# A 64-token chunk of the feed-forward block, split by output channels over both column halves of TensorE

## The chip, the cores and the metric

The kernel runs on one core of one Trainium2 chip. The metric is the device time of one execution, in microseconds (us), as the median of a few runs. Times from the profile come from one more execution, taken with the hardware profiler.

## What is computed

The input is 32 images of 56 x 56 positions with 128 channels, all float32. Two layers follow each other, each added to its input. The first is windowed attention (7 x 7 windows, shifted by 3, four heads) on a group-normalised input. The second is a Fourier layer: cosine transforms along both directions, 32 modes kept and mixed, transformed back, and then a feed-forward block on every token. The change touches the end of the second layer alone. Cut to what matters:

```
def _feedforward(x, W1, b1, W2, b2):          # W1: 128 x 512, W2: 512 x 128
    h = jax.nn.relu(x @ W1 + b1)
    return h @ W2 + b2

x = x + _L0_conv_ref(_gn(x), ...)             # attention
x = x + feedforward(forward_fourier(_gn(x)))  # Fourier layer; x here is the residual
```

## The kernel before, in words

The program walks over "cycles". A cycle does one row of eight windows (7 lines of an image) in each stage of the attention, and beside it one step of the Fourier layer of an image whose attention is over. An image takes eight cycles, and the stages of several rows and two images overlap in one cycle. The orders of TensorE (PE), ScalarE (ACT), VectorE (DVE) and GpSimd (POOL) are written out by hand: they run what the functions below emit, in the order of the program. SyncE's queue (SP) issues nearly all DMAs; its order is set by the framework's scheduler, which places each DMA by an estimate of when it can go, so it may move when the program changes.

An image has 3136 tokens. The feed-forward block takes them in seven groups, `FF_GROUPS = (512, 512, 512, 512, 512, 320, 256)`, in the cycles that `FF_AT` names, one group to a cycle. In this text the groups are numbered from 0; group 5 is the one with 320 tokens. Three functions do a group:

- `ff_in` (L816) issues the load of the residual `res` from the scratch tensor `scr` in DRAM, 128 tokens to a column block (L822), and of a last part of fewer tokens, if there is one (L826). It then does the first layer: for each of the four blocks f of 128 hidden units, TensorE makes W1's block times the tokens in a PSUM bank, and ScalarE writes it with bias and ReLU to `hid` (L833). The hidden units lie on the partitions, the tokens along the free axis.
- `ff_bias` (L836) has POOL add the output bias `b2sb` to `res` (L840).
- `ff_out` (L847) does the second layer into one PSUM bank `pf`. For each chunk of 128 tokens and each f, the stationary operand is `hid` (128 hidden units x 128 tokens) and the moving operand is W2's block `wff2[:, f]` (128 x 128 channels). The tokens come out on the partitions. VectorE adds `pf` and `res` (L868), and SP stores the result (L880, L881, L888).

All matmuls of this block go through `halved`:

```
    def halved(dst, lhsT, rhs, start=True, stop=True):
        for p in range(0, dst.shape[0], P // 2):
            ps = slice(p, min(p + P // 2, dst.shape[0]))
            nc.tensor.matmul(dst[ps], lhsT=lhsT[:, ps], rhs=rhs, start=start, stop=stop)
```

It cuts the stationary operand into two of 64 columns, one for each half of the array's columns; the halves' results lie on partitions 0 to 63 and 64 to 127. All matmuls of this kind stand under line L113 in the profile.

Group 5 has two chunks of 128 tokens and one of 64. The chunk of 64 needs only one piece in `halved`, on partitions 0 to 63: four matmuls of 64 stationary columns and 128 moving columns.

In a cycle with a feed-forward group, TensorE runs around `ff_out` in this order: attention values (L546), scores (L477), the transform back (L789), the value product (L455), `ff_out` (L113), the attention's projection (`attn_project`, L591), q and k of the next row (L113, tile `xw`), and the next group's `ff_in` (L113, tile `xf`). VectorE follows with the output add (L868), the projection's residual add (L599), the softmax sums (L507, L509), and the statistics (L616, L629; the squares in between are ScalarE's L628). One other group of matmuls matters for comparison: `fourier_stats` (L649) multiplies a fixed 128 x 128 matrix, cut into halves of 64 columns, with 64 moving columns, twice per image.

The image normalisation (`image_norm`, L362) uses a small VectorE tile `gmeans` (L383), which the change also touches.

Of the kernel before, what the change touches and what calls it, by code (L numbers as in the profile page):

```python
# [9 lines left out]
F32 = mybir.dt.float32  # L10
AF = mybir.ActivationFunctionType
ALU = mybir.AluOpType
AX = mybir.AxisListType

P = 128
S = 56
C = 128
WS = 7
SS = 3
# [5 lines left out]
NT = S * S  # L25
NM = 32
FF = 512
NF = FF // P
# [5 lines left out]
JP = 64  # L34
HB = 512

HALVES = (slice(0, P // 2), slice(P // 2, P))
# [3 lines left out]
FF_GROUPS = (HB, HB, HB, HB, HB, 320, 256)  # L41
# [6 lines left out]
def swin_fourier_kernel(  # L48
# [20 lines left out]
    nc = tc.nc  # L69
    NB = x.shape[0]  # L70

    const = ctx.enter_context(tc.tile_pool(name="const", bufs=1))
    big = ctx.enter_context(tc.tile_pool(name="big", bufs=1))
    work = ctx.enter_context(tc.tile_pool(name="work", bufs=2))
    small = ctx.enter_context(tc.tile_pool(name="small", bufs=2))
# [6 lines left out]
    def attn_bank():  # L82
        return bank("pa", 4)

    def conv_bank():
        return bank("pc", 4)
# [22 lines left out]
# [5 lines that stand above are left out]
# [153 lines left out]
    b1sb = const.tile([P, NF], F32, tag="b1sb", name="b1sb")  # L267
    wff2 = const.tile([P, NF, C], F32, tag="wff2", name="wff2")
    b2sb = const.tile([P, C], F32, tag="b2sb", name="b2sb")

    def ff_weights():
        nc.sync.dma_start(wff1, W1)
        nc.sync.dma_start(b1sb, b1.rearrange("(f p) -> p f", p=P))
        nc.sync.dma_start(wff2, W2.rearrange("(f p) o -> p f o", p=P))
        nc.sync.dma_start(b2sb, b2.partition_broadcast(P))

    mhalf = const.tile([P, 1], F32, tag="mhalf", name="mhalf")
    nc.gpsimd.memset(mhalf, -0.5)
# [83 lines left out]
    def image_norm(im):  # L362

        GR = C // 16

        def average(out, src):
            sums = small.tile([P, GR], F32, tag="gsums", name="gsums", bufs=2)
            nc.vector.tensor_reduce(
                sums, src.rearrange("p (g c) -> p g c", c=4), axis=AX.X, op=ALU.add
            )  # L370
            nc.vector.tensor_scalar(
                out.rearrange("p (g c) -> p g c", c=4),
                sums.unsqueeze(2).to_broadcast([P, GR, 4]),
                0.25,
                None,
                ALU.mult,
            )

        nc.vector.bn_aggr(stat[:, 0:2], im.st)

        turned = small.tile([P, 32], F32, tag="turned", name="turned", bufs=2)
        nc.vector.transpose(turned, stat)
        mean = small.tile([P, 2, 32], F32, tag="gmeans", name="gmeans", bufs=2)  # L383
        average(mean[:, 0], turned)
        yield
        nc.vector.tensor_tensor(turned, turned, mean[:, 0], ALU.subtract)
        nc.vector.tensor_tensor(turned, turned, turned, ALU.mult)
        average(mean[:, 1], turned)
        back = small.tile([P, 2, 32], F32, tag="back", name="back", bufs=2)
        nc.vector.transpose(  # L390
            back.rearrange("p k c -> p (k c)"), mean.rearrange("p k c -> p (k c)")
        )
        gm = back[:, 0, 0:1]

        im.mean = small.tile([P, 1], F32, tag="mean0", name="mean0")
        nc.vector.tensor_scalar(im.mean, gm, -1.0, None, ALU.mult)

        ve = small.tile([P, 1], F32, tag="ve", name="ve")
        nc.vector.scalar_tensor_tensor(
            out=ve, in0=back[:, 0, 1:2], scalar=1e-5, in1=back[:, 1, 0:1], op0=ALU.add, op1=ALU.add  # L400
        )
        rstd = small.tile([P, 1], F32, tag="rstd0", name="rstd0")
        nc.gpsimd.tensor_tensor(rstd, ve, mhalf, ALU.pow)
        im.w = work.tile([P, 3 * C], F32, tag="wn", name="wn")
        im.bias = small.tile([P, 5], F32, tag="bqkv", name="bqkv")
        yield
        nb = small.tile([P, 1], F32, tag="nb0", name="nb0")
        nc.vector.scalar_tensor_tensor(
            out=nb, in0=gm, scalar=-1.0, in1=rstd, op0=ALU.mult, op1=ALU.mult
        )  # L410
        nc.scalar.mul(im.w, wqkv, rstd)  # L411
        yield
        pb = attn_bank()
        halved(pb[:, 0:1], wqkv[:, 2 * C :], nb)
        nc.vector.tensor_copy(im.bias[:, 2:3], pb[:, 0:1])
        yield
# [399 lines left out]
    def ff_in(im, g):  # L816
        t0, n = sum(FF_GROUPS[:g]), FF_GROUPS[g]
        k, last = n // P, n % P
        xff = im.xf.rearrange("p r w -> p (r w)")
        scr_tok = im.scr.rearrange("h w c -> (h w) c")  # L820
        res = work.tile([P, 4, C], F32, tag="res", name="res")
        nc.sync.dma_start(  # L822
            res[:, :k], scr_tok[t0 : t0 + k * P].rearrange("(n p) c -> p n c", p=P)
        )
        if last:
            nc.sync.dma_start(res[:last, k], scr_tok[t0 + k * P : t0 + n])  # L826
        im.res = res
        im.hid = []
        for f in range(NF):
            ph = conv_bank()  # L830
            halved(ph[:, :n], wff1[:, f * P : (f + 1) * P], xff[:, t0 : t0 + n])
            hf = work.tile([P, HB], F32, tag="hid", name="hid", bufs=NF)
            nc.scalar.activation(hf[:, :n], ph[:, :n], AF.Relu, bias=b1sb[:, f : f + 1])  # L833
            im.hid.append(hf)

    def ff_bias(im, g):  # L836
        k, last = FF_GROUPS[g] // P, FF_GROUPS[g] % P
        for c0, c1, m in ((0, k, P), (k, k + 1, last)):
            if m:
                nc.gpsimd.tensor_tensor(  # L840
                    im.res[:m, c0:c1],
                    im.res[:m, c0:c1],
                    b2sb[:m].unsqueeze(1).to_broadcast([m, c1 - c0, C]),
                    ALU.add,
                )

    def ff_out(im, g):  # L847
        t0, n = sum(FF_GROUPS[:g]), FF_GROUPS[g]
        k, last = n // P, n % P
        res = im.res  # L850
        out_tok = out[im.b].rearrange("h w c -> (h w) c")
        chunks = [P] * k + ([last] if last else [])
        pf = conv_bank()
        for c, m in enumerate(chunks):
            for f in range(NF):
                halved(
                    pf[:m, c * C : (c + 1) * C],
                    im.hid[f][:, c * P : c * P + m],
                    wff2[:, f],
                    start=(f == 0),  # L860
                    stop=(f == NF - 1),
                )
        parts = [(0, k, P), (k, k + 1, last)]
        if im.b == NB - 1 and g == len(FF_GROUPS) - 1:
            parts = [(c, c + 1, m) for c, m in enumerate(chunks)]
        for c0, c1, m in parts:
            if m:
                nc.vector.tensor_tensor(  # L868
                    res[:m, c0:c1],
                    pf[:m, c0 * C : c1 * C].rearrange("p (n c) -> p n c", c=C),  # L870
                    res[:m, c0:c1],
                    ALU.add,
                )

        c = 0
        while c < len(chunks):
            m = chunks[c]
            o = t0 + c * P + SS * S
            if o < NT < o + m:
                nc.sync.dma_start(out_tok[o:NT], res[: NT - o, c])  # L880
                nc.sync.dma_start(out_tok[: o + m - NT], res[NT - o : m, c])  # L881
                c += 1
                continue
            e = c + 1
            while len(parts) == 2 and e < len(chunks) and chunks[e] == m and (o >= NT or o + (e + 1 - c) * m <= NT):
                e += 1
            o %= NT
            nc.sync.dma_start(  # L888
                out_tok[o : o + (e - c) * m].rearrange("(n p) c -> p n c", p=m), res[:m, c:e]
            )  # L890
            c = e

    images = {}  # L900
# [78 lines left out]
    def behind_max(cycle):  # L979
        if cycle % NWR == NWR - 1:  # L980
            norm_step(cycle)
        turn(cycle)
        for im, c in fourier(cycle):
            if c == 0:
                next(im.stats, None)
            if c in FF_AT:
                ff_bias(im, FF_AT.index(c))
        last, j = row(cycle - 4)
        if last and j < NWR - 1:
            add_sums(last, j)  # L990
        next_groups(cycle)
# [115 lines left out]
    def last_out(cycle):  # L1107
        for im, c in fourier(cycle):
            if c in FF_AT:
                ff_out(im, FF_AT.index(c))  # L1110
# [34 lines left out]
    def first_rows(cycle):  # L1145
# [47 lines left out]
        if cycle == 8:  # L1193
            ff_weights()
# [116 lines left out]
```

## Time and profile before

| what | value |
|---|---|
| median of 3 runs | 3284.2 us (3283.5 to 3284.87) |
| the profiled execution's own time | 3282.72 us |
| its span, from first to last instruction | 3280.9 us |
| mean granted TensorE clock | 0.991 |
| busy share of TensorE, its weight loads, VectorE, ScalarE, POOL | 96, 73, 80, 64, 72% |
| moved by DMA | 448.39 MB, 137 GB/s |

Each row of the groups names a line of the kernel, the engine, the operation, the tiles written and read with their shapes, and the count; then the total busy time and the mean duration of one; then how long the engine sat idle just before these instructions, and what ended that. PE stands for matmuls, PEld for TensorE's weight loads, which run beside them. A matmul's duration is that of a pipeline and longer than the distance to the next one, so distances between starts say more than durations. A float32 matmul appears as two matmul records and two weight-load records. In the chain of waits, "issue" is time in which the engine waited for nothing that the profile shows. Queue q8 in the page carries TensorE's instructions.

### The profile page before, as it was taken

To read this page: it belongs to the slowest core of one execution; us is meant where nothing else is said; L and a number is where in the kernel's file an instruction comes from. 1 tells how busy PE (TensorE), PEld (TensorE's weight loads), DVE (VectorE), ACT (ScalarE), POOL (GpSimd) and SP (SyncE) were. 2 spreads that over 40 slices of the span, in tenths; PEclk is the share of its full clock that TensorE was granted. 3 is DMA by queue.
4 is the path that set the end of the run, shared out by engine and by line. 5 is a ranking of instruction groups with operands and counts; after the bars stand their busy time and mean duration, and the time that the engine had idled before them with its cause. 6 is when DMAs were issued, how large, how long until landed. Compare 5 with 4: busy or idle time off the path is not lost.

```text
span 3280.9 us, 151050 instructions
## 1 busy us (share of the span) xinstructions
PE 3154.8 (96%) x65408; PEld 2394.1 (73%) x65408; DVE 2637.5 (80%) x5066; ACT 2100.4 (64%) x3680; POOL 2346.8 (72%) x2634
## 2 busy tenths in 40 slices
PE   4689999999999999999999999999999999999999
PEld 3467777777777777777777777777777777777776
DVE  8788888888888888888888888888888888888751
ACT  3456766666766666666666766666666666666663
POOL 7777777777777677777777777777777777777741
PEclk9799999999999999999999999999999999999999
DMA  6546556565556555656556656656565656565453
GB/s 115 106 119 147 137 138 144 136 143 146 137 134 142 137 142 143 142 135 146 137 144 145 141 134 143 137 141 144 136 140 136 146 131 146 140 143 136 121 140 96
DMA packets 1168157, 448.39 MB, mean 137 GB/s; under 512 B 520106, under 2 KB 1137628, under 8 KB 1167492
## 3 DMA queue, kind: packets, MB, share of 16 engines
q1 hardware_dynamic: 1158148, 433.18, 55.7%
q8 instruction: 514, 8.42, 1.1%
q10 hardware_dynamic: 8736, 5.38, 0.7%
q14 instruction: 151, 1.24, 0.1%
q0 software_dynamic: 608, 0.17, 0.0%
HBM read 276.97 MB, written 161.48 MB: 134 GB/s over the span
## 4 chain that ended last, share of the span: by engine, by line
PE 83%; ACT 7%; DVE 3%; DMA 2%; issue 2%; SPq 2%; POOL 0%; ACTq 0%; DVEq 0%; POOLq 0%
PE pc L113 38%; PE pa L113 10%; PE pa L455 7%; PE pc L789 5%; PE pa L591 5%; PE pc L750 5%; PE pa L477 5%; PE pa L546 4%; PE pc L702 3%; ACT hid L833 2%; ACT k L442 2%; SPq L760 1%; ACT xr L628 1%; ACT z L758 1%; DMA zscr<-z 1%
## 5 line engine op out<-in xcount | busy, mean ns | idle before, releaser
L521 POOL TENSOR_TENSOR blocks<-a,rs 128x512 f32<-128x512 f32 x1506 | 1280.5, 857 | 399.2 <-DVE rs L509 251.2
L113 PE MATMUL pc<-wff,hid 128*64 128x128 f32 x12544 | 742.0, 273 | 2.6 <-ACT hid L833 1.0
L113 PE MATMUL pc<-xf,wff 128*64 128x512 f32 (+2 forms) x3584 | 718.5, 539 | 1.0 <-DVE xf L807 0.9
L113 PEld LDWEIGHTS pc<-wff,hid 128*64 128x64 f32 x12544 | 706.5, 137 | 15.7 <-ACT hid L833 5.3
L496 POOL TENSOR_TENSOR a<-a,mx 128x784 f32<-128x784 f32 x251 | 377.7, 1505 | 358.6 <-DVE mx L495 341.6
L113 PEld LDWEIGHTS pc<-xf,wff 128*64 128x64 f32 x3584 | 278.6, 136 | 356.8 <-issue 249.6
L833 ACT ACTIVATE hid<-pc,b1sb 128x512 f32<-128x512 f32 (+2 forms) x896 | 500.5, 643 | 41.1 <-PE pc L113 41.1
L113 PE MATMUL pa<-xw,wn 128*64 128x392 f32 x2048 | 399.9, 501 | 29.6 <-ACT wn L411 29.6
L462 ACT COPY v<-pa 128x512 f32<-128x512 f32 x256 | 151.9, 593 | 414.7 <-PE pa L455 411.7
L485 DVE TENSOR_TENSOR a<-pa,bm 128x392 f32<-128x392 f32 x502 | 260.0, 559 | 90.2 <-PE pa L477 70.8
L442 ACT ACTIVATE k<-pa,bqkv,heads 128x392 f32<-128x392 f32 x512 | 319.0, 674 | 14.9 <-PE pa L113 1.1
L840 POOL TENSOR_TENSOR res<-res,b2sb 128x512 f32<-128x512 f32 (+2 forms) x256 | 265.7, 1044 | 85.0 <-DMA res<-scr 85.0
L725 ACT ACTIVATE y<-modes,rstd 128x448 f32<-128x448 f32 x256 | 276.3, 1137 | 71.5 <-DVE modes L718 64.0
L531 DVE STREAM_TRANSPOSE eT<-blocks 128x1024 f32<-128x1024 f32 x256 | 313.4, 1224 | 0.9 <-POOL blocks L521 0.9
L502 ACT ACTIVATE a<-a 128x784 f32<-128x784 f32 x251 | 214.9, 856 | 151.1 <-POOL a L496 150.9
L455 PE MATMUL pa<-wn,xw 128*64 128x128 f32 x4096 | 289.1, 283 | 22.0 <-ACT oT L578 16.4
L127 POOL TENSOR_TENSOR xr<-xr,bproj 128x384 f32<-128x384 f32 (+1 forms) x256 | 292.6, 1143 | 20.6 <-DMA xr<-in_x_dram 7.9
L546 PEld LDWEIGHTS pa<-eT,v 49*32 49x32 f32 x16384 | 173.6, 106 | 161.1 <-ACT hid L833 48.7
L432 ACT ACTIVATE q<-pa,bqkv 128x392 f32<-128x392 f32 x256 | 149.3, 583 | 220.7 <-PE pa L113 219.0
L576 DVE TENSOR_SCALAR oT<-pa,bqkv 128x147 f32<-128x147 f32 (+2 forms) x768 | 171.5, 279 | 140.5 <-PE pa L546 138.3
L507 DVE TENSOR_REDUCE sm<-a 128x16 f32<-128x784 f32 x251 | 240.9, 960 | 40.2 <-ACT a L502 40.1
L591 PE MATMUL pa<-wproj,oT 128*64 128x128 f32 x3584 | 249.9, 275 | 23.3 <-DVE oT L576 21.1
(108 smaller groups left out, 4975.3 us busy)
## 6 DMA issues: line engine op xcount, KB each, us to landing
zscr<-z SPq DMA_DIRECT2D x512, 112.0 KB
xin<-in_x_dram SPq DMA_DIRECT2D x496, 112.0 KB
htok<-scr SPq DMA_DIRECT2D x256, 196.0 KB
zT<-zscr SPq DMA_DIRECT2D x192, 256.0 KB
res<-scr SPq DMA_DIRECT2D x160, 256.0 KB
out_dram<-res SPq DMA_DIRECT2D x160, 256.0 KB
scr<-x SPq DMA_DIRECT2D x256, 112.0 KB
xr<-in_x_dram SPq DMA_DIRECT2D x256, 84.0 KB
```

Source lines behind the costliest of these rows:

```text
L113: nc.tensor.matmul(dst[ps], lhsT=lhsT[:, ps], rhs=rhs, start=start, stop=stop)
L127: nc.gpsimd.tensor_tensor(piece, piece, bproj.unsqueeze(1).to_broadcast([P, n, C]), ALU.add)
L442: nc.scalar.activation(k_sb[:, u], pk[:, :RT].rearrange("p (w j) -> p w j", j=WT), AF.Identity, bias=im.bias[:, 3 + u : 4 + u], scale=head ...
L455: nc.tensor.matmul(pv[HALVES[w % 2], w // 2 * C : (w // 2 + 1) * C], lhsT=im.half[i // NP][:, t0 : t0 + JP], rhs=im.w[:, 2 * C : 3 * C], s ...
L496: nc.gpsimd.tensor_tensor(a3, a3, mx.unsqueeze(2).to_broadcast([P, 2 * NWR, WT]), ALU.subtract)
L521: nc.gpsimd.tensor_tensor(dst[to, k, :, :n], a3[src, :, kb * KB : kb * KB + n], rs[src].unsqueeze(2).to_broadcast([src.stop - src.start, 2 ...
L531: nc.vector.transpose(eT.rearrange("p t (k j) -> p k t j", k=2), blocks[r % 2])
L546: nc.tensor.matmul(po4[u][h * HD : (h + 1) * HD, pr], lhsT=v[ks, pr, h * HD : (h + 1) * HD], rhs=eT[ks, h * NP + pr, :WT], start=True, sto ...
L591: nc.tensor.matmul(pp[hs, (n - n0) * C : (n - n0 + 1) * C], lhsT=oT[:, t0 : t0 + JP], rhs=wproj, start=True, stop=True,)
L725: nc.scalar.mul(y[:, r], t.rearrange("p (n k) -> p n k", k=NM), im.rstd)
L833: nc.scalar.activation(hf[:, :n], ph[:, :n], AF.Relu, bias=b1sb[:, f : f + 1])
L840: nc.gpsimd.tensor_tensor(im.res[:m, c0:c1], im.res[:m, c0:c1], b2sb[:m].unsqueeze(1).to_broadcast([m, c1 - c0, C]), ALU.add,)
```

## The change

The 64 tokens of the last chunk of group 5 are kept on all 128 partitions: partitions 0 to 63 hold channels 0 to 63 of the 64 tokens, and partitions 64 to 127 hold channels 64 to 127 of the same tokens. For each f there are now two matmuls, one per half of the array's columns, with the same stationary operand (the 64 tokens of `hid`) and 64 moving columns each, in place of one with 128 moving columns. The residual part is loaded by two DMAs, one per channel half, the bias comes from a new tile `b2half` that holds the bias in that layout (loaded once, by two DMAs), the adds of POOL and VectorE run on 128 x 64 elements, and two DMAs store the part. The tile `gmeans` has one buffer instead of two. The other edits of `ff_bias` and `ff_out` write the loops over full chunks apart from the last part and leave what they issue as it was; blank lines after `ff_out` are gone.

```
+    b2half = const.tile([P, JP], F32, tag="b2half", name="b2half")
...
+        for hs in HALVES:
+            nc.sync.dma_start(b2half[hs], b2[hs].partition_broadcast(JP))
...
-        mean = small.tile([P, 2, 32], F32, tag="gmeans", name="gmeans", bufs=2)
+        mean = small.tile([P, 2, 32], F32, tag="gmeans", name="gmeans", bufs=1)
...
         if last:
-            nc.sync.dma_start(res[:last, k], scr_tok[t0 + k * P : t0 + n])
+            for hs in HALVES:
+                nc.sync.dma_start(res[hs, k, :JP], scr_tok[t0 + k * P : t0 + n, hs])
...
     def ff_bias(im, g):
...
+        if last:
+            part = im.res[:, k, :JP]
+            nc.gpsimd.tensor_tensor(part, part, b2half, ALU.add)

     def ff_out(im, g):
...
-        for c, m in enumerate(chunks):
+        for c in range(k):
             for f in range(NF):
                 halved(
-                    pf[:m, c * C : (c + 1) * C],
-                    im.hid[f][:, c * P : c * P + m],
+                    pf[:, c * C : (c + 1) * C],
+                    im.hid[f][:, c * P : (c + 1) * P],
                     wff2[:, f],
                     start=(f == 0),
                     stop=(f == NF - 1),
                 )
+        if last:
+            for f in range(NF):
+                for hs in HALVES:
+                    nc.tensor.matmul(
+                        pf[hs, k * C : k * C + JP],
+                        lhsT=im.hid[f][:, k * P : k * P + JP],
+                        rhs=wff2[:, f, hs],
+                        start=(f == 0),
+                        stop=(f == NF - 1),
+                    )
...
+        if last:
+            part = res[:, k, :JP]
+            nc.vector.tensor_tensor(part, pf[:, k * C : k * C + JP], part, ALU.add)
...
+        if last:
+            o = (t0 + k * P + SS * S) % NT
+            for hs in HALVES:
+                nc.sync.dma_start(out_tok[o : o + JP, hs], res[hs, k, :JP])
```

More of the change, by code (lines that the diff above doesn't have):

```diff
@@ L837, in ff_bias @@
         k, last = FF_GROUPS[g] // P, FF_GROUPS[g] % P
[L838 to L845, printed above, removed]
+        nc.gpsimd.tensor_tensor(
+            im.res[:, :k],
+            im.res[:, :k],
+            b2sb.unsqueeze(1).to_broadcast([P, k, C]),
+            ALU.add,
+        )
+        if last:
+            part = im.res[:, k, :JP]
+            nc.gpsimd.tensor_tensor(part, part, b2half, ALU.add)
     def ff_out(im, g):
@@ L851, in ff_out @@
         out_tok = out[im.b].rearrange("h w c -> (h w) c")
-        chunks = [P] * k + ([last] if last else [])
         pf = conv_bank()
-        for c, m in enumerate(chunks):
+        for c in range(k):
             for f in range(NF):
                 halved(
-                    pf[:m, c * C : (c + 1) * C],
-                    im.hid[f][:, c * P : c * P + m],
+                    pf[:, c * C : (c + 1) * C],
+                    im.hid[f][:, c * P : (c + 1) * P],
                     wff2[:, f],
@@ L862, in ff_out @@
                 )
[L863 to L873, printed above, removed]
+        if last:
[7 more added lines that the diff above has]
+                        stop=(f == NF - 1),
+                    )
+        alone = im.b == NB - 1 and g == len(FF_GROUPS) - 1
+        parts = [(c, c + 1) for c in range(k)] if alone else [(0, k)]
+        for c0, c1 in parts:
+            nc.vector.tensor_tensor(
+                res[:, c0:c1],
+                pf[:, c0 * C : c1 * C].rearrange("p (n c) -> p n c", c=C),
+                res[:, c0:c1],
+                ALU.add,
+            )
+        if last:
+            part = res[:, k, :JP]
+            nc.vector.tensor_tensor(part, pf[:, k * C : k * C + JP], part, ALU.add)
         c = 0
-        while c < len(chunks):
-            m = chunks[c]
+        while c < k:
             o = t0 + c * P + SS * S
-            if o < NT < o + m:
+            if o < NT < o + P:
                 nc.sync.dma_start(out_tok[o:NT], res[: NT - o, c])
-                nc.sync.dma_start(out_tok[: o + m - NT], res[NT - o : m, c])
+                nc.sync.dma_start(out_tok[: o + P - NT], res[NT - o :, c])
                 c += 1
@@ L884, in ff_out @@
             e = c + 1
-            while len(parts) == 2 and e < len(chunks) and chunks[e] == m and (o >= NT or o + (e + 1 - c) * m <= NT):
+            while not alone and e < k and (o >= NT or o + (e + 1 - c) * P <= NT):
                 e += 1
@@ L888, in ff_out @@
             nc.sync.dma_start(
-                out_tok[o : o + (e - c) * m].rearrange("(n p) c -> p n c", p=m), res[:m, c:e]
+                out_tok[o : o + (e - c) * P].rearrange("(n p) c -> p n c", p=P), res[:, c:e]
             )
             c = e
+        if last:
+            o = (t0 + k * P + SS * S) % NT
+            for hs in HALVES:
+                nc.sync.dma_start(out_tok[o : o + JP, hs], res[hs, k, :JP])
     images = {}
```

## The prediction

> **What bounds the kernel now.** I read the page first: engine shares, then the slices, then the groups.
>
> ```profile
> span 3280.9 us, 151050 instructions
> PE 3154.8 (96%) x65408; PEld 2394.1 (73%) x65408; DVE 2637.5 (80%) x5066; ACT 2100.4 (64%) x3680; POOL 2346.8 (72%) x2634
> PE   4689999999999999999999999999999999999999
> ...
> L113 PE MATMUL pc<-wff,hid 128*64 128x128 f32 x12544 | 742.0, 273 | 2.6 <-ACT hid L833 1.0
> ...
> q8 instruction: 514, 8.42, 1.1%
> ```
>
> Only TensorE is full, and the few tenths it lacks are in the first three slices. Busy time by stretch puts a number on that (columns: length, then busy us and instructions of PE, PEld, DVE, ACT, POOL):
>
> ```profile
> 120.00:3160.00 3040.00, 2979.19 (x62569) 2268.78 (x62570) 2515.67 (x4803) 2004.35 (x3518) 2244.75 (x2499) 0.99 0.58 139
> ```
>
> In the steady part it is busy 2979 of 3040 us, 98%. So TensorE time taken out of that part comes off the end, if no other engine becomes late. A busy record is not a full array, though: the group above is the second layer of the feed-forward block, and each of its matmuls fills one half of the array's columns. A float32 matmul is two records, so a 128-token chunk is 4 f x 2 halves x 2 = 16 records, and the 64-token chunk of group 5 is 8 records, all in the same half. The chain of waits for group 6 (two full chunks), then the order in time at group 5 (two and a half):
>
> ```profile
> 314.71 1.75 PE pc L113 x32
> ```
>
> ```profile
> 304.10 2.67 PE L113 MATMUL pc<-wff,hid 128*64 128x128 f32 x39
> 306.51 0.32 PE L591 MATMUL pa<-wproj,oT 128*64 128x128 f32 x1
> 306.61 0.27 PE L113 MATMUL pc<-wff,hid 128*64 128x128 f32 x1
> 306.67 0.76 PE L591 MATMUL pa<-wproj,oT 128*64 128x128 f32 x10
> 307.21 0.49 PE L113 MATMUL pa<-xw,wn 128*64 128x392 f32 x1
> 307.26 0.27 PE L591 MATMUL pa<-wproj,oT 128*64 128x128 f32 x1
> ```
>
> 32 records in 1.75 us are 16 pairs of 109.2 ns: both halves work, a pair at a time. Record by record, the last 8 starts of group 5 stand singly 109.1 ns apart (7 intervals in 764 ns, in all 32 images): a single costs what a pair costs, and the other half idles. It is used for only a moment: the projection's first matmul in that half (306.51) overtakes the chunk's last record (306.61). That lead of some 160 ns is not a gain: the halves' starts stay staggered through L113's next two groups (54 and 161 ns apart in the second), and the value product at 310.51 starts only after the later half. So the chunk costs 8 x 109.2 = 874 ns of the critical half.
>
> [...]
>
> **The change, part by part.**
>
> *Matmuls.* 4 matmuls of 128 columns in one half become 8 of 64 columns, alternating: 16 records instead of 8, in 8 pairs. Does a pair of 64 columns cost half of a pair of 128, with its weight loads? One group in this trace has this shape:
>
> ```profile
> L649 PEld LDWEIGHTS pa<-tot,gmean x128: 132/137/137, 127.3 to 3170.3; 128*64 128x64 f32 x128
> L649 PE MATMUL pa<-tot,gmean x128: 219/222/270, 127.3 to 3170.4; 128*64 128x64 f32 x128
> ```
>
> There are four pairs an image, each with its own loads, halves alternating as in the new code. Their starts are 56, 59 and 58 ns apart (172 or 173 ns over three intervals in 27 of 32 images). In the chain the eight records take 0.23 us, 57 ns a pair. A load starts 2 ns after the matmul before it in its half, and the next matmul 55 ns after that, so the load is hidden. I take 58 ns: 8 x 58 = 464 ns, against 874, saves 410 ns an image, and the halves stay together. Times 32: 13.1 us. [...]
>
> *Does it pass on?* The wait that ends last here is on TensorE itself. Behind the chunk come the projection, the next row's q and k, and the first layer of group 6; none waits more than a few ns now. VectorE is full at that place (4.50 of 4.50 us from 304.0 to 308.5), so its two L868 adds, at 307.09 when TensorE had been done 0.2 us, cannot start 0.41 us sooner. But at 310.75 it idles 1.02 us for ScalarE's squares (L628), which wait behind q and k, and so on TensorE: they come sooner by the 0.41, and VectorE catches up in its idle time. If that cover were gone, some 0.2 us an image (6 us) would be lost.
>
> *Adds and bias.* The part goes from 64x128 to 128x64:
>
> ```profile
> L868 DVE TENSOR_TENSOR res<-pc,res 64x128 f32<-64x128 f32 x32 | 8.7, 273 | 0.0
> ...
> L868 DVE TENSOR_TENSOR res<-pc,res 128x256 f32<-128x256 f32 x63 | 26.3, 418 | 57.3 <-POOL res L840 37.0 <-PE pc L113 15.5 <-issue 4.8
> ```
>
> 128 more elements cost 145 ns, so half the row saves about 70 ns of VectorE; POOL's L840 (452 ns for the 64x128, 732 for the 128x256) saves about 140. Both lie beside TensorE: nothing.
>
> *DMA.* Load and store of the part become two each: 2 issues more an image on SP's queue (some 0.4 us each; the load of the part takes 456 ns to issue), 128 packets of 256 B instead of 64 of 512 B each way. Packets of both sizes average about 30 ns in the records (27 and 31), so 2 x 64 x 30 ns / 16 engines is 0.24 us of a 98 us image. The part is loaded at 299.27 and first used at 305.71; half a microsecond more leaves 5. In SP's order one input load (xin, for a later image's quarter) moves behind six loads of xr, some 4 us; the last of that quarter's loads is issued at 411.49 and the quarter is turned at 432.72. The two zT loads that follow have 7 us until their use (402.24 to about 409.9). Nothing. The two b2half loads fall in the start, while the queue holds other constants: nothing. The single gmeans buffer is written and read by VectorE alone, in order: nothing.
>
> *Instruction fetch.* The image's period, from group 5 to group 5, is 97.93 us in half of the images and up to 100.7 in others; over 28 periods the excess is 18.8 us. It is stalls like this one in the chain:
>
> ```profile
> 902.01 1.51 PE pc L789 x59
> 903.52 0.62 issue
> 904.14 0.41 PE pc L789 x5
> ```
>
> The stall ends 1.4 us after a q8 packet landed, and nearly all that come and go with the image do so within 1.3 to 1.8 us. An image has 4115 TensorE instructions, 16 x 256 + 19, so the 256-boundary moves by 19 each image, and the excess is a smooth function of its place: nearly 0 over some 40% of the circle, up to 2.7 us at the worst. The change adds 4 matmuls of 4 instructions: the step becomes 35. Reading the measured excess at the new places gives 19.6 to 21 us for 28 periods: 1 to 2 us lost, I take 1.6.
>
> *Sum.* -13.1 + 1.6 = -11.5 us. The profiled execution took 3282.7 us (span 3280.9 and 1.8 around it), so 3271.2; the median is 1.5 higher: 3272.7 us, 0.35% faster.
>
> **Rivals.** 0.2%, 6.6 us, is about what a measurement of this kernel can tell from no change.
>
> A, weight loads show (12%): in a run of eight short pairs the loads no longer hide[...]. For it: the value product L546 needs some 95 ns a round of its eight tiles[...]. Against: L649 has the very shape, at 58. At 95 ns: 32 x 8 x 14 ns = 3.6 us saved, 2 lost to fetch: 3282.6 us. The same result follows if VectorE's cover fails and half is lost.
>
> B, fetch stalls grow (5%, ends slower): the boundary falls in the dense stretches (L546, L477, L789) more often than the interpolation says. It decides from 0.4 us an image, where it eats all 13.1 us; to be slower by 0.2% it must add 0.6 us to today's 0.67 an image. At 1.4 us an image, half of the worst, it adds 23 us: 3284 - 13 + 23 = 3294 us. Against: the walk still visits the whole circle.
>
> C, the forecast (83%): 3272.7; own range 3269 to 3277.
>
> **Numbers.** The likeliest case is C. [...] High end: pairs at 70 ns (10 us saved) with 4 us of stalls, 3278. C reaches beyond 6.6 us gained nearly always, so faster 0.82; same 0.13, mostly A; slower 0.05, B.
>
> **What would show it.** Right: the last 16 records of group 5 in pairs 58 ns apart; no projection record ahead of them; the images without fetch stalls at 97.52 us instead of 97.93; L868's part near 200 ns; stalls summing to some 20 us. Wrong: pairs over 75 ns; or pairs at 58 but 97.93 us kept, with a new wait on VectorE or on zT; or the same short period with more time between the images.

## The result and the profile after

| | before | changed | ratio, 95% interval |
|---|---|---|---|
| first comparison, 6 runs each | 3285.72 us | 3274.7 us | 0.9965 [0.9953, 0.9978] |
| second, on another occasion, 30 and 6 runs | 3281.86 us | 3271.1 us | 0.9969 [0.9957, 0.9981] |
| third, 9 and 5 runs | 3286.1 us | 3275.2 us | 0.9968 [0.9955, 0.998] |

The forecast was 3272.7 us, 0.35% less. The changed kernel is 0.31 to 0.35% faster, about 11 us each time. One of the 30 executions of the kernel before (4549 us, at a granted clock of 0.654) and one of the experiment before_dma (8012 us) ran far slower than the rest and are left out of the ratios. The profiled execution took 3275.91 us, with a span of 3274.1. From its page, the span, the engine shares, the group of full chunks and the instruction queue:

```profile
span 3274.1 us, 151714 instructions
...
PE 3147.8 (96%) x65664; PEld 2369.2 (72%) x65664; DVE 2637.3 (81%) x5066; ACT 2099.2 (64%) x3680; POOL 2340.5 (71%) x2634
...
q8 instruction: 516, 8.45, 1.2%
...
L113 PE MATMUL pc<-wff,hid 128*64 128x128 f32 x12288 | 715.3, 273 | 2.4 <-ACT hid L837 1.0
```

The full chunks now have 12288 records under L113: the 256 of the short chunk (8 in each of 32 images) have left this group. They come back as 512 of their own. The instruction queue gives the 256 that the prediction counts in: before, 514 packets of 16 KB for 131703 TensorE instructions in the trace (65408 matmuls, 65408 weight loads, 887 others), now 516 for 132215. That is 256.2 a packet in both, and 512 instructions more are two packets more. The rows of the groups that belong to the part of 64 tokens, shapes kept apart (matmuls, POOL's bias, VectorE's add):

```profile
L870 PE MATMUL pc<-wff,hid 128*64 128x64 f32 x512 | 20.7, 222 | 0.0
...
L850 POOL TENSOR_TENSOR res<-res,b2half 128x64 f32<-128x64 f32 x32 | 10.3, 322 | 0.2 <-DMA res<-scr 0.2
L888 DVE TENSOR_TENSOR res<-pc,res 128x64 f32<-128x64 f32 x32 | 6.9, 214 | 0.0
```

The chain of waits of the changed kernel in the first image, at group 5 (start, length, what):

```profile
305.35 1.75 PE pc L113 x32
307.10 0.47 PE pc L870 x16
307.56 0.66 PE pa L594 x12
308.22 1.32 PE pa L113 x8
309.54 1.73 PE pc L113 x16
```

The two full chunks take 1.75 us as before; the short one takes 0.47 us in 16 records. The order in time shows that the array's halves stay together: the chunk's 16 records stand in one piece and the projection (L594) begins behind them.

```profile
305.18 1.92 PE L113 MATMUL pc<-wff,hid 128*64 128x128 f32 x32
306.93 0.64 PE L870 MATMUL pc<-wff,hid 128*64 128x64 f32 x16
307.39 0.83 PE L594 MATMUL pa<-wproj,oT 128*64 128x128 f32 x12
308.05 1.49 PE L113 MATMUL pa<-xw,wn 128*64 128x392 f32 x8
```

Record by record, the 8 pairs of the chunk start 56 to 59 ns apart in this image, and each pair's two records 6 or 7 ns apart. In 29 of the 32 images the mean distance is 58.0 ns; the other three, with 58.3 to 79.9, raise the mean over all to 58.9.

For the whole I take the records from one image's first matmul of group 5 to the next image's: 28 such periods lie in the part where attention and feed-forward run side by side. The shortest is an image without stalls; the sum of what the others have over it is called the excess. (Counted from 97.92 us, not 97.93 as in the prediction, it is 19.2 us for the kernel before.)

| profiled execution | shortest period, us | excess over 28, us | first group 5 at, us |
|---|---|---|---|
| before | 97.92 | 19.2 | 304.1 |
| changed, first | 97.51 | 24.2 | 305.2 |
| changed, second | 97.53 | 18.1 | 304.6 |
| changed, third | 97.52 | 21.3 | 305.8 |

In the first pair of profiles, 28 x 0.41 = 11.5 us are gained, 5.0 go to a larger excess and 1.1 to a later start; after the last of the 28 periods 1.4 us are gained. That is 6.8 us, the difference of the two spans. Why the start-up differs by up to 1.7 us between profiles was not looked into. The medians differ by more, 11 us. One pair of profiles can't be expected to tell that closely: the excess of the changed kernel alone lies between 18.1 and 24.2 us in its three profiles.

### The profile page after: what moved, and what is told of

The parts are those of the page before. It is cut to its first block, busy times and chain, and to the rows that moved or that the text cites. A ratio compares the mean times of both kernels' runs of the same rounds, so it can differ in the third digit from the quotient of the medians.

```text
span 3274.1 us, 151714 instructions
## 1 busy us (share of the span) xinstructions
PE 3147.8 (96%) x65664; PEld 2369.2 (72%) x65664; DVE 2637.3 (81%) x5066; ACT 2099.2 (64%) x3680; POOL 2340.5 (71%) x2634
## 4 chain that ended last, share of the span: by engine, by line
PE 84%; ACT 7%; DVE 2%; issue 2%; DMA 2%; SPq 2%; POOL 1%; ACTq 0%; DVEq 0%; POOLq 0%
PE pc L113 38%; PE pa L113 10%; PE pa L458 8%; PE pc L792 5%; PE pa L594 5%; PE pa L480 5%; PE pc L753 5%; PE pa L549 4%; PE pc L705 3%; ACT hid L837 2%; ACT k L445 2%; SPq L763 1%; ACT xr L631 1%; ACT z L761 1%; DMA zscr<-z 1%
## 5 line engine op out<-in xcount | busy, mean ns | idle before, releaser
L113 PE MATMUL pc<-wff,hid 128*64 128x128 f32 x12288 | 715.3, 273 | 2.4 <-ACT hid L837 1.0
L113 PE MATMUL pc<-xf,wff 128*64 128x512 f32 (+2 forms) x3584 | 714.5, 539 | 1.1 <-DVE xf L810 0.9
L113 PEld LDWEIGHTS pc<-wff,hid 128*64 128x64 f32 x12288 | 679.6, 137 | 15.0 <-ACT hid L837 5.3
L113 PEld LDWEIGHTS pc<-xf,wff 128*64 128x64 f32 x3584 | 267.1, 136 | 368.1 <-issue 254.5
L113 PE MATMUL pa<-xw,wn 128*64 128x392 f32 x2048 | 397.6, 503 | 30.2 <-ACT wn L414 29.7
L445 ACT ACTIVATE k<-pa,bqkv,heads 128x392 f32<-128x392 f32 x512 | 318.6, 674 | 15.4 <-PE pa L113 1.3
L842 POOL TENSOR_TENSOR res<-res,b2sb 128x512 f32<-128x512 f32 (+1 forms) x224 | 252.3, 1126 | 87.5 <-DMA res<-scr 87.5
L458 PEld LDWEIGHTS pa<-wn,xw 128*64 128x64 f32 x4096 | 227.6, 140 | 62.0 <-ACT oT L581 29.0
```

Of the source, the lines that this page charges most:

```text
L445: nc.scalar.activation(k_sb[:, u], pk[:, :RT].rearrange("p (w j) -> p w j", j=WT), AF.Identity, bias=im.bias[:, 3 + u : 4 + u], scale=head ...
L458: nc.tensor.matmul(pv[HALVES[w % 2], w // 2 * C : (w // 2 + 1) * C], lhsT=im.half[i // NP][:, t0 : t0 + JP], rhs=im.w[:, 2 * C : 3 * C], s ...
L842: nc.gpsimd.tensor_tensor(im.res[:, :k], im.res[:, :k], b2sb.unsqueeze(1).to_broadcast([P, k, C]), ALU.add,)
```

## Experiments

**The changed kernel again** (after_again and after_third), beside the others:

> The changed kernel once more, so that the others can be read against it on one chip. Theory (the chunk's pairs of 58.8 ns in both halves of the array take the place of singles of 109.2 ns): 0.9965 of the kernel before, some 11 us less, with 97.5 us as the shortest image period. Rival (the gain of the first comparison was mostly the chip's scatter): under 5 us.

> The changed kernel a third time, as the reference on the same chip for the two beside it: ratio 0.9965 to 0.997, shortest image period 97.5 us, an excess of 18 to 24 us over 28 periods.

Measured: 3271.1 and 3275.2 us, ratios 0.9969 and 0.9968. The gain is no scatter, and the three profiles' shortest periods lie within 0.03 us.

**The same matmuls, one half after the other** (half_order).

```
-            for f in range(NF):
-                for hs in HALVES:
+            for hs in HALVES:
+                for f in range(NF):
```

> The changed kernel with the same eight matmuls of the chunk in another order: the four of the first column half, then the four of the second. Theory (the gain is that both halves work at the same time): each half's 8 records run alone at about 58 ns, 928 ns in all less some 120 ns by which the second half can run ahead, so about 340 ns an image or 11 us are lost again, and the time is that of the kernel before, ratio 0.998 to 1.001. Rival (it is the shorter matmuls or the other layout of loads, adds and stores that gain, whatever the order): as the changed kernel, ratio 0.9965.

Measured: 3279.89 us, ratio 0.9995 [0.9987, 1.0004]: 8.8 us over the changed kernel beside it, and not to be told from the kernel before. The shortest period is 97.82 us, 0.3 more than the changed kernel's and 0.1 less than that of the kernel before. Its order in time at the chunk:

```profile
307.48 0.74 PE L870 MATMUL pc<-wff,hid 128*64 128x64 f32 x13
308.00 0.32 PE L594 MATMUL pa<-wproj,oT 128*64 128x128 f32 x1
308.06 0.28 PE L870 MATMUL pc<-wff,hid 128*64 128x64 f32 x2
308.16 0.27 PE L594 MATMUL pa<-wproj,oT 128*64 128x128 f32 x1
```

The picture of the kernel before is back: a projection record in the free half overtakes the chunk's last ones. Instructions, shapes, adds and DMAs, and the single gmeans buffer, are those of the changed kernel; only the order differs. Some three quarters of the 0.4 us an image are lost by the order alone. So it is the two halves at work at once that gains, and not the shorter matmuls nor the layout. Four matmuls of 64 columns in each half cost, one half after the other, little less than four of 128 in one half: by the periods some 0.77 us against 0.87. Sixteen records singly at 58 ns would be 928 ns, so by the periods some 0.16 us of them were done ahead, an estimate; 0.12 were expected.

**The chunk twice** (twice): the eight matmuls are repeated over the same bank.

```
-            for f in range(NF):
+            for f in [*range(NF), *range(NF)]:
```

> The changed kernel with the chunk's eight matmuls done twice, the second time over the first. Theory (TensorE's time at this place reaches the end one to one): 16 records in 8 pairs of 58.8 ns more, 0.47 us an image, 15 us in all over the changed kernel, so about 3290 us, ratio 1.001, shortest image period 97.98 us; instruction-fetch stalls as before within 3 us. Rival (VectorE is full at this place and sets the pace there, so the time of TensorE counts in part only): under 8 us over the changed kernel.

Measured: 3291.03 us, ratio 1.0028 [1.0018, 1.0038], 19.9 us over the changed kernel. The chain at the chunk:

```profile
305.01 0.93 PE pc L870 x32
```

0.93 us for 32 records is twice 0.47. The shortest period is 97.99 us, 0.45 more: some 15 us in 32 images, nearly one to one, so VectorE's fullness here does not damp it. The other 5 us were not expected: the excess is 24.4 us against 18.1, a growth of 6.3 where I allowed 3.

**The DMA side alone, in the kernel before** (before_dma).

```
-            nc.sync.dma_start(res[:last, k], scr_tok[t0 + k * P : t0 + n])
+            for hs in HALVES:
+                nc.sync.dma_start(res[:last, k, hs], scr_tok[t0 + k * P : t0 + n, hs])
...
+            if m < P:
+                for hs in HALVES:
+                    nc.sync.dma_start(out_tok[o : o + m, hs], res[:m, c, hs])
+                c = e
+                continue
```

> The kernel before with only the DMA side of the change: the 64-token part is loaded and stored in two DMAs of 64 channels each (packets of 256 B) instead of one. Theory (transfers and SyncE's queue have slack): no change, ratio 1.000 within 0.001, and the same shortest image period of 97.93 us. Rival (the two more issues and shorter packets cost part of the gain): slower by 2 us or more, 1.0007 and up.

Measured: 3283.19 us against 3281.86, ratio 1.0001 [0.9993, 1.001]; shortest period 97.93. The excess is 20.9 us. The shorter packets and the two more issues cost nothing that can be measured, though the interval reaches to 3 us and so does not quite exclude the rival's 2.

**Where the excess comes from.** The next largest term of the prediction is the instruction fetch. First attempt: make an image's number of TensorE instructions a multiple of 256, nearly, so that the boundary between instruction packets (256 instructions each, by the q8 rows above) stays where it is from image to image. Group 4's first layer is cut into pieces of 64 tokens (`pieces` gives their number). Two kernels, fetch_quiet and fetch_loud, differ only in the first image, which places the boundary. The diff is that of fetch_quiet; the last line is the one that fetch_loud has instead.

```
-            halved(ph[:, :n], wff1[:, f * P : (f + 1) * P], xff[:, t0 : t0 + n])
+            w = wff1[:, f * P : (f + 1) * P]
+            step = n // pieces(im, g, f)
+            for s in range(0, n, step):
+                halved(ph[:, s : s + step], w, xff[:, t0 + s : t0 + s + step])
...
+        if g == 4:
+            return 8
+        return 8 if im.b == 0 and g == 3 else 1
...
+        return (8, 4, 1, 1)[f] if im.b == 0 and g == 3 else 1
```

> The changed kernel with the first layer of group 4 done in pieces of 64 tokens instead of 512: the same products, 56 more matmuls an image, 224 more TensorE instructions, so that an image has 4355 = 17 x 256 + 3 of them and the 256-instruction boundary hardly moves from image to image. In the first image group 3 is cut up as well, which sets the boundary to where the changed kernel's trace shows no stalls. Theory (the images' excess over the shortest period is TensorE waiting for instruction packets): the pieces cost 8 x 58.8 - 429 = 41 ns a record and half, 0.33 us an image, so a shortest period of 97.85 us, but the excess over 28 periods falls from 23.7 us to under 6: 3262 to 3268 us in all, ratio 0.993 to 0.995. Rival (the excess comes from late data transfers, zT above all): the excess stays near 24 us and the time is the changed kernel's plus 10 us, 3285 us, ratio 1.000.

> The same as the one with the boundary in the quiet place, but with group 3 of the first image cut up less (80 instructions instead of 224, once), so that the boundary stays where the changed kernel's trace shows stalls of 1 to 3 us an image. Every other image's work is the same. Theory (instruction packets): an excess of 30 to 50 us over 28 periods, some 40 us slower than the quiet one, 3300 to 3315 us, ratio 1.005 to 1.009. Rival (late data transfers): the same time as the quiet one within 3 us.

Measured: 3301.52 us, ratio 1.0059 [1.0042, 1.0076], and 3312.02 us, ratio 1.0095 [1.008, 1.011]. Both expectations for the quiet one failed; the loud one fits its own, but the two are only 10.5 us apart, not 40. The shortest periods are 98.19 and 98.07 us (97.85 expected), the excess over them 31.3 and 46.5 us. What happened stands in the waits of TensorE's matmuls between 320 and 3160 us (total us, times, longest), first of the changed kernel, then of fetch_quiet:

```profile
PE pc L792 <- issue: 10.1, 12, 1.4
PE pa L458 <- issue: 4.8, 9, 1.0
```

```profile
PE pc L792 <- issue: 26.7, 27, 2.3
```

In fetch_quiet nearly every image stalls once, nearly always at the transform back (L792) 83 to 86 us after group 5, right behind group 4's first layer. The sites of the changed kernel's stalls at 10 and 22 to 24 us have gone silent. So the boundary was where I wanted it. But the changed kernel stalls in some images at 83 to 88 us too, and it is there that group 4's 256 instructions in pieces of 64, followed by the attention values and scores, now make a dense stretch. That the density makes the stall is a reading of the place; no run of its own tests it. Of some 38 us of gaps that are over 0.15 us longer than usual, 36 end 1.1 to 1.9 us after an instruction packet landed.

Second attempt: the 224 instructions are spread over groups 1 to 3, whose cycles have few instructions otherwise, in larger pieces (fetch_pad); the boundary goes where all profiles so far had hardly a stall, before and after the middle of the image.

```
+        if g == 3:
+            return 2 if im.b or f < 2 else 1
+        return 4 if g in (1, 2) else 1
```

> The changed kernel with the first layer of groups 1 and 2 in pieces of 128 tokens and of group 3 in pieces of 256: the same products, 224 more TensorE instructions an image, 4355 = 17 x 256 + 3, spread over three cycles that are not dense in instructions. In the first image two blocks f of group 3 stay whole, which sets the boundary to the places where all runs so far show hardly a stall, before and after the middle of the image. Theory (stalls are waits for instruction packets where the boundary falls in a dense stretch): pieces cost 62 + 62 + 25 = 150 ns an image, shortest period 97.67 us, but the excess over 28 periods falls from some 20 us to under 7; 8 to 16 us faster than the changed kernel, ratio to the kernel before 0.992 to 0.994. Rival (any more instructions are fetched at the cost of stalls elsewhere, as in the first attempt): an excess of 18 us or more, and slower than the changed kernel by 4 us or more.

And the same from the other side, by fewer instructions (fetch_whole): nine first-layer matmuls an image are not cut into halves.

```
+        if g == 3:
+            return im.b and f == 0
+        return g == 1 or (g == 2 and im.b > 0)
...
+            if whole(im, g, f):
+                nc.tensor.matmul(ph[:, :n], lhsT=w, rhs=xff[:, t0 : t0 + n], start=True, stop=True)
+            else:
+                halved(ph[:, :n], w, xff[:, t0 : t0 + n])
```

> The changed kernel with nine first-layer matmuls an image (groups 1 and 2, one of group 3) not cut into column halves: 36 TensorE instructions fewer, 4095 = 16 x 256 - 1 an image; in the first image only four, which sets the boundary to a quiet place. Theory (instruction packets): excess under 5 us over 28 periods. What the whole matmuls cost is not shown by any trace here: [...]I take 0.3 us. So 6 to 18 us faster than the changed kernel, ratio 0.9915 to 0.995. Rival (late data transfers): excess as in the changed kernel, 18 us or more.

Measured: fetch_pad 3255.13 us, ratio 0.9911 [0.9898, 0.9925], shortest period 97.60, excess 1.7 us. fetch_whole 3266.37 us, ratio 0.994 [0.9928, 0.9953], shortest period 97.89, excess 2.1 us. fetch_pad is 20.1 us faster than the changed kernel beside it, more than the 8 to 16 expected; fetch_whole is 8.8 us faster, within its 6 to 18; the 0.3 us an image that its whole matmuls were to cost was my estimate from no trace, and its shortest period is 0.37 longer. In the waits of fetch_pad's matmuls over the same stretch, no "issue" is left; the largest is one on ScalarE that the changed kernel has too (14.1 us):

```profile
PE pa L458 <- ACT oT L581: 14.7, 28, 0.5
PE pc L113 <- ACT xf L815: 0.3, 1, 0.3
PE pc L113 <- DVE xf L810: 0.2, 1, 0.2
```

One kernel issues 224 instructions more and the other 36 fewer, and both lose the excess, with the same loads of zT, the transform back's input. Late transfers are out as its cause.

The profiles of the kernels without pieces say the same. In the three of the changed kernel, every gap between matmuls that is more than 0.2 us longer than usual at its place (24.2, 15.4 and 19.2 us in sum) ends 1.1 to 1.9 us after an instruction packet landed. The excess repeats image by image: its correlation between two profiles with the same number of instructions is 0.90 (before and before_dma), 0.85 and 0.87 (the changed kernel's first with its second and third). Count the TensorE instructions recorded up to the first matmul of an image's group 5. Where they are 64 to 127 more than a multiple of 256, the mean excess of such images is under 0.2 us in each of these five profiles; at 224 to 255 more it is 1.5 to 2.2 us.

**The chunk's worth with the stalls out of both** (before_pad and fetch_pad_again). The kernel before gets pieces too, 240 more instructions, for the same 4355 an image.

```
+        if g == 3:
+            return (4 if f == 0 else 2) if im.b else (2 if f < 2 else 1)
+        return 4 if g in (1, 2) else 1
```

> The kernel before with its first layer cut into pieces in the same manner (groups 1 and 2 in pieces of 128, group 3 in pieces of 256 and one block of it in 128), 240 more TensorE instructions an image, so that it too has 4355 = 17 x 256 + 3 and the boundary stays in the quiet place. Theory: shortest period 97.92 + 0.08 = 98.0 us, excess under 4 us, so 16 us faster than the kernel before, ratio 0.995; and 0.40 us an image, 13 us, slower than the changed kernel with pieces beside it: the chunk's own worth with the fetch stalls out of both. Rival (the change is worth what the first comparison showed, 11 us, and fetch had no part in the difference to 13.1): 11 us or less between the two.

> The changed kernel with pieces once more, as the reference for the kernel before with pieces: ratio 0.991, shortest period 97.6 us, excess under 3 us, 13 us faster than the one beside it.

Measured: 3270.68 us, ratio 0.9964 [0.995, 0.9977], and 3256.76 us, ratio 0.9923 [0.991, 0.9935]: 13.9 us apart, with five runs each that spread over 3.8 and 3.7 us. Shortest periods 98.04 and 97.64, excess 2.4 and 1.6 us. The chunk's worth is thus 0.40 us an image, as with the stalls in. The 13.9 us fit the forecast 13.1 better than the rival's 11 or less, but fetch_pad stood 4 us nearer to the kernel before here than on the first occasion (0.9923 against 0.9911), so the medians alone don't settle 2 us. For the kernel before, the pieces are worth 13.0 us.

## Why the prediction was right

*Matmuls.* Eight pairs of 58 ns were forecast from the statistics' group L649; 58.0 were measured in 29 of 32 images, and 0.38 to 0.41 us less in the shortest period, against 0.41. The weight loads stay hidden in a run of eight pairs as in one of four: at L870 a load mostly starts 1 to 3 ns after the matmul before it in its half, and the next matmul 54 to 56 ns after the load. With the stalls out of both kernels the change is worth 13.9 us by the medians, 13.1 by the forecast. Half_order shows the cause. That the old chunk's overtaking record was no gain is seen from the size of the saving: it is nearly the whole 874 - 464 = 410 ns, with nothing to deduct for the overtaking.

*Passing on.* The 0.41 us an image reach the end, and an added 0.45 us does too (twice). VectorE at group 5, first in the kernel before, then in the changed one:

```profile
307.09 0.60 DVE L868 TENSOR_TENSOR res<-pc,res 128x256 f32<-128x256 f32 x2
...
310.75 0.55 DVE L629 TENSOR_REDUCE part<-xr 128x32 f32<-128x384 f32 x1 [1.02 <-ACT xr L628]
```

```profile
308.18 0.41 DVE L880 TENSOR_TENSOR res<-pc,res 128x256 f32<-128x256 f32 x1
308.50 0.21 DVE L888 TENSOR_TENSOR res<-pc,res 128x64 f32<-128x64 f32 x1
...
311.43 0.55 DVE L632 TENSOR_REDUCE part<-xr 128x32 f32<-128x384 f32 x1 [0.68 <-ACT xr L631]
```

Counted from group 5's first matmul (304.10 before, 305.18 now) the add starts at 3.00 us, as before (2.99): as forecast, it does not come sooner. The sums behind the squares start at 6.25 us instead of 6.65, and the idle time ahead of them has shrunk from 1.02 to 0.68 us. That is the cover, and it was large enough.

*Adds, bias, DMA.* VectorE's part takes 214 ns against 273 (59 less; about 70 forecast), POOL's 322 against 452 (130; 140 forecast). Two more DMAs each way cost nothing (before_dma). The input load that slips behind six others in SyncE's order did not show in the shortest period; VectorE waits longer for inputs in all (26.2 us against 15.5 on the first line concerned), but no matmul waits for that line, and weight loads wait 0.9 us for it in all.

*Instruction fetch.* The reading was right: nearly all of the excess goes with the instruction packets, its size with where the 256-boundary falls (18.1 to 24.2 us in the changed kernel's three profiles, 1.7 in fetch_pad and 2.1 in fetch_whole). Forecast was a loss of 1 to 2 us, 1.6 taken. The first profile shows 5.0, the three together a mean excess of 21.2 against 19.2, so 2.0. But before_dma, which has the TensorE instructions of the kernel before, shows 20.9, and half_order, which has those of the changed one, 19.1. With scatter of this size the term is between nothing and some 3 us: it fits the forecast, and is not confirmed to the microsecond. That the sum came within half a microsecond of the measured gain (11.5 forecast, 11.0 measured) is in part luck. The low end of the own range, 3269 us, was my estimate; no trace shows it.

*Rivals.* A (loads show) is out: pairs at 58.0 ns. That L546's rounds wait for weight loads was not shown. (What the prediction calls the value product, here and at 310.51, is L546, the attention values.) B (fetch stalls grow) did not occur in this change, but fetch_quiet shows that it can: 224 more instructions an image, badly placed, cost about 30 us against the changed kernel (0.9% between the ratios), of which 11 were forecast for the pieces themselves.

## What to carry to other kernels

A short last chunk that fills half of the array's columns cost as much here as a full one (874 ns); cutting its output channels, not its tokens, over both halves gave nearly half of that back, because the two halves alternate in the order of issue (58.0 ns a pair; in half_order, one half after the other, 0.3 us an image were lost again) and TensorE is what ends last. In a kernel that is bound by TensorE and repeats one long body, look at the "issue" waits: if they walk from place to place over the repetitions, compare the number of TensorE instructions in the body with a multiple of what a packet holds, 256 here (131703 instructions in 514 packets). Making it nearly one, with the boundary where the traces showed hardly a stall, was here worth 13.0 us in the kernel before and 20.1 in the changed one, as much as the change itself or more: with both, 3255.13 us, 0.9911 of the kernel before. Where the boundary falls has to be measured: three of the forecasts here (twice, fetch_quiet, fetch_pad) missed the excess or the time.

## What the runs showed of the hardware that was not expected

- A stall of TensorE that waits for nothing visible, 0.6 to 0.9 us an image in the mean and up to 3.4 in the two kernels compared, goes with one number: the place of the instruction count modulo 256. It repeats between profiles of the same count (correlation 0.85 to 0.90). Its total is 18 to 24 us where the count moves by 19, 35 or 67 an image, and about 2 where it moves by 3 or 255 with the boundary in a quiet place.
- With 224 instructions added in group 4's first layer alone, TensorE stalls 27 times at the same line for 1 us each (fetch_quiet); the same number added elsewhere leaves an excess of 1.7 us (fetch_pad).
- In fetch_whole, first-layer matmuls over all 128 columns run at the same rate as two halves (429 ns a record), but the second record of each whole group starts 533 ns after the first: 104 ns a group, and three groups make most of the 0.37 us by which fetch_whole's shortest period is longer.
